# A feed-forward residual formed on token rows by GpSimd and added by VectorE in a stream of encoder jobs

## The chip, the core and the metric

The kernel runs on one core of one Trainium2 chip. The core has a matrix engine (TensorE, "PE" in the profile, with its weight loads as "PEld"), a vector engine (VectorE, "DVE"), a scalar engine (ScalarE, "ACT"), a general engine (GpSimd, "POOL") and a queue that only issues transfers (SyncE, "SP"). Products land in PSUM, which this part of the kernel uses as eight banks of 128 x 512 float32. The metric is the device time of one execution in microseconds (us); less is better. Before the change it is 2834.29 us, the median of three runs (2834.08 to 2835.43).

## The reference, cut to what matters

The reference is a chain of sixteen residual blocks on 2048 tokens of width 128, which the kernel holds as 8 images of 256 rows. The change touches one kind of block, `_L3_ffn_ref`, which is applied twice, once before and once after a sliding-window attention. It is a mixture of four encoder layers, of which a gate picks two for each image:

```python
def _encoder_layer(x, iw, ib, ow, ob, l1w, l1b, l2w, l2b, n1w, n1b, n2w, n2b):
    qkv = x @ iw.T + ib
    q, k, v = ...                      # 16 heads of width 8
    attn = softmax(q @ k.T / sqrt(8))
    o = (attn @ v) @ ow.T + ob
    x = _layernorm(x + o, n1w, n1b)
    ff = relu(x @ l1w.T + l1b) @ l2w.T + l2b
    return _layernorm(x + ff, n2w, n2b)
gate_logits = x.mean(axis=1) @ gate_w.T + gate_b
# the two best experts per image, weighted by the softmax over all four
return einsum('be,ebsd->bsd', gate_weights * mask, expert_outs)
```

The residual in question is the `x + ff` of the last line of `_encoder_layer`, where `x` is the normalised and scaled output of the first layer norm.

## The kernel before

**Jobs and passes.** `tail` runs the last stages as one stream, a `StripAttention`. Its queue holds 40 jobs: 16 encoder jobs (8 images x 2 experts), 8 window-attention jobs, 16 encoder jobs again. Attention over 16 heads is done in four strips of query columns, and the stream advances in passes, `s = 0, 1, 2, ...`, four per job. `burst(s)` issues, for the job of pass `s`, the four score tiles (`ps_s`, one per group of 32 rows, line 154), and for the strip two passes back the four weight tiles (`ps_t`, line 154). They go in two halves: two score and two weight tiles first, then the other two of each. Every tile is a bank of PSUM of 512 columns, taken from one ring of eight (`sml`), and it is written in two column blocks: the program lists the first blocks of all four tiles of a half, then the second blocks. After each half come the row maxima of its score tiles on VectorE (`top`, line 178, written to `nsp`) and the exponentials of its weight tiles on ScalarE (line 201, written to `g_pt`).

**Hooks.** All other work is hung on a pass with an order number and is issued after the pass's tiles in that order: the value product of an earlier strip (`av`, `ps_o`, order 1), the projections q, k, v of jobs ahead (`ps_q`, `ps_k`, `ps_v`, order 3), the normalisation (`half`, order 6), and last `lower` (order 9), which turns the maxima (`ps_m`) and adds them to the queries on VectorE (`qa`, line 209). A job begins at pass `4n`; its attention output is normalised seven passes later, and its feed-forward part runs beside the attention of the next jobs.

**Order.** In this stage the four compute engines keep the order in which the program issues their instructions (`manual_schedule`). What the planner still decides is which of the eight banks a tile takes, and it adds the semaphore waits that follow: a tile that takes a bank waits for the last reader of the tile that held it.

**The feed-forward part** is `ExpertFeed`, with these hooks for job `i` (pass counted from the job's first, order in brackets):

- 6 (0) `fetch`, line 818: gathers `g_ring` (the two weight matrices) and `g_RC` (263 columns of vectors) from device memory by an indirect transfer that GpSimd issues.
- 10 (0) `first_roots`: statistics of the first norm on VectorE, roots on GpSimd; 11 (8) `norm`: ScalarE writes the normalised rows `gxh`.
- 12 (5) `turn`, lines 858 to 870: TensorE turns `gxh` (`g_t`), ScalarE scales it to `gy` (features on partitions, line 866), and GpSimd adds the second bias to it as `gyr` (line 869).
- 13 and 14 (7) `up`: `g_h` = first weights x `gy` (line 876), ScalarE's ReLU to `g_hs`.
- 15 and 16 (7) `down`, lines 884 to 899: for each half of the rows, `g_f` is accumulated from an identity product of `gyr` (line 888), which puts the residual in, and four products of `g_hs` (line 892). ScalarE copies it out to `g_tt` (line 899).
- 16 and 17 (0) `second_roots`, lines 901 to 911: VectorE's statistics of `g_tt` (lines 904, 905) and its scaling (line 906), then roots on GpSimd. 18 (8) `settle`, lines 913 to 920: GpSimd weighs the result and adds it to `x`.

`open_` in `encoder_job` gathers the attention's weights `g_A` and vectors `g_RA`, both at once, at order 0 six passes before the job (for the first four jobs, at hooks of the stage before). `ps_q` needs `g_A` two passes later.

Of the kernel before, what the change touches and what calls it, by code (L numbers as in the profile page):

```python
# [15 lines left out]
ALU = mybir.AluOpType  # L16
# [3 lines left out]
P = 128  # L20
D = 128
B = 8
T = 256
# [786 lines left out]
class ExpertFeed:  # L810
# [4 lines left out]
    def tile(self, shape, name, bufs=2):  # L815
        return self.net.sa.wk.tile(shape, F32, tag=name, name=name, bufs=bufs)

    def fetch(self, i):
        w = self.net.gring[:, i % 4, :]
        self.gather_rows(None, "g_B", i, out=w)  # L820
        self.st[i] = dict(w=w, r=self.gather_rows(self.net.sa.wk, "g_RC", i, 4))

    def roots(self, mv, name, wi=None):
        nc = self.nc
# [34 lines left out]
    def turn(self, i):  # L859
        nc, d = self.nc, self.st[i]  # L860
        r = d["r"]
        ps = self.net.sml("g_t")
        for u in range(2):
            nc.tensor.transpose(ps[:, u * P : (u + 1) * P], d["xh"][:, u, :], self.net.ident)
        d["y"], d["yr"] = self.tile([P, T], "gy"), self.tile([P, T], "gyr")
        nc.scalar.activation(
            d["y"], ps[:, :T], AF.Identity, bias=r[:, 261:262], scale=r[:, 260:261]
        )
        nc.gpsimd.tensor_scalar(d["yr"], d["y"], r[:, 262:263], None, ALU.add)
        d["h"] = self.tile([P, 4, T], "g_hs")  # L870

    def up(self, i, a):
# [11 lines left out]
    def down(self, i, u):  # L884
        net, nc, d = self.net, self.nc, self.st[i]
        ps = net.sml("g_f")
        sl = slice(u * P, (u + 1) * P)
        nc.tensor.matmul(
            out=ps[:, :D], lhsT=d["yr"][:, sl], rhs=net.ident, start=True, stop=False
        )  # L890
        for j in range(4):
            nc.tensor.matmul(  # L892
                out=ps[:, :D], lhsT=d["h"][:, j, sl], rhs=d["w"][:, 512 + j * D : 512 + (j + 1) * D],
                start=False, stop=j == 3,
            )
        if u == 0:
            d["st"], d["mv"] = self.tile([P, 2, 6], "g_st2", 2), self.tile([P, 2, 2], "g_mv2", 2)
            d["t"] = self.tile([P, 2, D], "g_tt", 3)
        nc.scalar.copy(d["t"][:, u, :], ps[:, :D])

    def second_roots(self, i, u):
        nc, d = self.nc, self.st[i]
        mv, t = d["mv"], d["t"][:, u, :]
        nc.vector.bn_stats(out=d["st"][:, u, :], in_=t)
        nc.vector.bn_aggr(out=mv[:, u, :], in_=d["st"][:, u, :])
        nc.vector.scalar_tensor_tensor(
            t, t, mv[:, u, 0:1], d["r"][:, 0:D], ALU.subtract, ALU.mult
        )
        if u:
            d["rs"] = self.roots(mv, "g_rs2")  # L910
            nc.gpsimd.tensor_scalar(d["rs"], d["rs"], self.wf[:, i : i + 1], None, ALU.mult)
# [290 lines left out]
class Net:  # L1202
# [988 lines left out]
    def tail(self):  # L2191
        nc = self.nc
        pe = mybir.EngineType.PE
        with ExitStack() as es:
            rt = es.enter_context(self.tc.tile_pool(name="g_r", bufs=1))
            wg = es.enter_context(self.tc.tile_pool(name="g_w", bufs=4))
            gates = [Gate(self, rt, e) for e in range(2)]
            sa = self.sa = StripAttention(self, None, None)
            for i in range(2 * B):
                sa.add(self.encoder_job(wg, gates[0], i), i > 3)  # L2200
            hooks = []
            for b in range(B - 1):
                hooks += [
                    (8 * b + 16, self.ln_roots, b), (8 * b + 18, self.ln_apply, b),
                    (8 * b + 20, self.ln_turn, b),
                ]
            for b0, b1 in ((0, 2), (2, 5)):
                s = 8 * b1 + 13
                hooks.append((s, gates[0].means, b0, b1))
                hooks += [(s + 3, f) for f in gates[0].choose(b0, b1)]  # L2210
            for i in range(4):
                hooks.append((57 + 2 * i, sa.jobs[i].begin))
            with self.banks("h", 2, 4):
                self.layernorm_stats()
                with self.tc.tile_pool(name="h_k", bufs=2) as wk:
                    with self.tc.manual_schedule(engines={pe}):
                        WideAttention(self, wk, self.xnT).run(hooks)
            es.enter_context(self.banks("g", big=0, sml=8))
            wk = es.enter_context(self.tc.tile_pool(name="g_a", bufs=2))
            pts = [  # L2220
                self.w16.tile([P, 2, 4, 512], F32, tag="w16", name=f"g_pt{i}") for i in range(2)
            ]
            sa.wk, sa.weights = wk, lambda t: pts[t % 2][:, t // 2 % 2]
            self.gring = self.w16.tile([P, 4, 1024], F32, tag="w16", name="g_ring")
            es.enter_context(self.tc.manual_schedule(engines=INORDER))

            def gating(gate, s, b0, b1):
                sa.at(s, 0, gate.means, b0, b1)
                first, *rest = gate.choose(b0, b1)
                sa.at(s + 1, 5, first)  # L2230
                for k, f in enumerate(rest):
                    sa.at(s + 2 + k, 0, f)

            sa.at(-4, 0, self.ln_roots, B - 1)
            sa.at(-2, 0, self.ln_apply, B - 1)
            sa.at(-1, 5, self.ln_turn, B - 1)
            gating(gates[0], 0, 5, 8)
            for b in range(B):
                n = len(sa.jobs)
                sa.at(4 * n - 9, 0, self.ln_roots, b)  # L2240
                sa.at(4 * n - 8, 0, self.ln_apply, b)
                sa.at(4 * n - 6, 5, self.ln_turn, b)
                sa.add(self.window_job(wk, b))
                end = 4 * n + sa.AV["w"] + 7
                sa.at(end, 0, self.ln_roots, b)
                sa.at(end + 2, 0, self.ln_apply, b)
                sa.at(end + 3, 5, self.ln_turn, b)
                for b0, b1 in ((0, 2), (2, 5), (5, 8)):
                    if b1 == b + 1:
                        gating(gates[1], end + 4, b0, b1)  # L2250
            for i in range(2 * B):
                sa.add(self.encoder_job(wg, gates[1], i))
            sa.run()

    def window_job(self, wk, b):
# [15 lines left out]
    def encoder_job(self, wg, gate, i):  # L2271
        nc, b = self.nc, i // 2
        if gate.feed is None:
            gate.feed = ExpertFeed(self, gate)
        feed = gate.feed
        got = {}

        def open_():
            wa = got["wa"] = gate.gather(wg, "g_A", i, 4)
            ra = got["ra"] = gate.gather(wg, "g_RA", i, 4)  # L2280
            return (
                self.xnT[:, b, :], wa[:, 0:256], wa[:, 256:512], wa[:, 512:640], wa[:, 768:770],
                wa[:, 770:772], ra[:, 0:D],
            )

        def first(j):
            j.t = self.transpose2(j.wk, j.o, "oT8", self.nc.vector.tensor_copy)
            j.xr = j.wk.tile([P, 2, D], F32, tag="xr", name="xr")
            nc.gpsimd.tensor_tensor(
                j.xr, self.xn[:, 2 * b : 2 * b + 2, :],  # L2290
                got["ra"][:, D:].unsqueeze(1).to_broadcast([P, 2, D]), ALU.add,
            )

        def second(j):
            feed.add(i, j.xr, self.rowproj(j.t, got["wa"][:, 640:768], True))

        av = StripAttention.AV[None]
        hooks = [(av + 5, 4, first), (av + 6, 2, second)]
        for d, order, f, args in (
            (av + 3, 0, feed.fetch, ()), (av + 8, 8, feed.norm, ()), (av + 9, 5, feed.turn, ()),  # L2300
            (av + 10, 7, feed.up, (0,)), (av + 11, 7, feed.up, (1,)),
            (av + 12, 7, feed.down, (0,)), (av + 13, 7, feed.down, (1,)),
            (av + 7, 0, feed.first_roots, ()), (av + 13, 0, feed.second_roots, (0,)),
            (av + 14, 0, feed.second_roots, (1,)), (av + 15, 8, feed.settle, ()),
        ):
            hooks.append((d, order, lambda j, f=f, args=args: f(i, *args)))
        job = Job(None, 8 ** -0.5, open_, hooks)
        job.whole_q = True
        return job

    def resident(self):
# [85 lines left out]
def _cols(b):  # L2397
    return b.reshape(-1, P).T
# [6 lines left out]
def _layout(i):  # L2405
# [92 lines left out]
    for n in "qkv":  # L2498
# [11 lines left out]
    g = {n[len(p) :]: v for n, v in i.items() if n.startswith(p)}  # L2510
# [8 lines left out]
                axis=1,  # L2519
# [13 lines left out]
            for e in range(4)  # L2533
# [6 lines left out]
                [  # L2540
                    np.repeat(g["ln2_w"][e : e + 1], P, axis=0),
                    np.repeat(g["ln2_b"][e : e + 1], P, axis=0), _cols(g["lin1_b"][e]),
                    _cols(g["ln1_w"][e]), _cols(g["ln1_b"][e]), _cols(g["lin2_b"][e]),
                ],
                axis=1,
            )
            for e in range(4)
# [23 lines left out]
```

## Time and profile before

| What | Value |
|---|---|
| Median of three runs | 2834.29 us |
| The profiled execution: its own time, and its span | 2835.47 us, 2833.5 us |
| Granted TensorE clock, mean over the span | 0.943 |
| TensorE busy, whole span | 2485.3 us (88%) |
| VectorE, ScalarE, GpSimd busy, whole span | 1973.9, 1419.8, 1417.6 us |
| 1955 to 2270 us (first encoder stretch): TensorE, VectorE, ScalarE, GpSimd busy | 307.35, 235.46, 203.51, 184.67 us of 315 |
| 2270 to 2480 us (mostly window attention) | 194.99, 165.94, 118.84, 154.69 us of 210 |
| 2480 to 2834 us (second encoder stretch and the end) | 332.05, 248.56, 221.41, 219.12 us of 354 |

The profile is one execution, recorded instruction by instruction; the span is from its first to its last instruction. A row of the timeline or of a group names the line of the kernel, the engine, the operation, what is written and from what, and the shape. A bracket after a row is the time that the engine sat idle just before, with the instruction that ended the wait. Instructions of float32 matrix products appear twice per product. Ends of matrix products are modelled, so that the time of one is best read from the distance between starts.

### The profile page before, as it was taken

Reading aid. Unit: us, or ns where it says so; the run is one execution under the profiler, and the core shown is the slowest. Engines: PE = TensorE matmul, PEld = TensorE weight load, DVE = VectorE, ACT = ScalarE, POOL = GpSimd, SP = SyncE. Lnnn points to the kernel's source line nnn. Section 1 sums busy time; section 2 is a strip of 40 time slices with the busy share of each in tenths; the row PEclk is TensorE's granted clock in tenths of the full one; section 3 lists DMA queues with packets and bytes.
Section 4 is the critical chain, followed back from the end, with each engine's and each line's share of the span. In section 5 each row is a group of like instructions: output and inputs, shape, how many; then the busy total and the mean of one; then the engine's idle time right before and its main releaser. Section 6 shows DMA issues by size and latency. Waiting matters only on the chain.

```text
span 2833.5 us, 63773 instructions
## 1 busy us (share of the span) xinstructions
PE 2485.3 (88%) x25374; PEld 1779.3 (63%) x25374; DVE 1973.9 (70%) x4881; ACT 1419.8 (50%) x3300; POOL 1417.6 (50%) x1924
## 2 busy tenths in 40 slices
PE   6888769989689979795797599998999999999997
PEld 3444357756467767574465466675677777767775
DVE  5888856767757776553675377777777777887774
ACT  5666324446334343321563155554666665566664
POOL 3777559712198405222002244543466668746666
PEclk8999879999889989897898799999999999999998
DMA  3000000000000200003000300100121100012211
GB/s 106 1 1 1 33 1 1 1 1 2 3 1 1 88 3 2 1 27 47 5 2 33 45 1 1 31 1 1 45 69 52 53 30 3 25 52 63 64 56 35
DMA packets 41993, 69.99 MB, mean 25 GB/s; under 512 B 9176, under 2 KB 30561, under 8 KB 40929
## 3 DMA queue, kind: packets, MB, share of 16 engines
q0 software_dynamic: 12288, 42.14, 5.7%
q1 hardware_dynamic: 29408, 23.78, 2.7%
q8 instruction: 201, 3.29, 0.5%
q14 instruction: 96, 0.78, 0.1%
HBM read 58.82 MB, written 7.08 MB: 23 GB/s over the span
## 4 chain that ended last, share of the span: by engine, by line
PE 39%; DVE 5%; POOL 3%; DMA 1%; ACT 1%; issue 1%; POOLq 0%; ACTq 0%; DVEq 0%
PE ps_s L154 6%; PE ps_o L1475 5%; PE ps_t L154 5%; PE g_h L876 2%; PE h_o L502 2%; PE h_s L457 2%; PE h_t L487 2%; PE g_f L892 2%; PE h_p L416 2%; DVE nsp L178 2%; PE ps_m L207 1%; PE ps_ot L1485 1%; PE ps_q L1470 1%; PE ps_k L1470 1%; PE h_v L440 1%
## 5 line engine op out<-in xcount | busy, mean ns | idle before, releaser
L178 DVE TENSOR_REDUCE nsp<-ps_s 128x2 f32<-128x512 f32 x640 | 397.9, 684 | 91.6 <-PE ps_t L154 87.4
L154 PE MATMUL ps_t<-qa,k 32*128 32x256 f32 (+2 forms) x3584 | 423.1, 373 | 7.1 <-DVE qa L209 4.7
L154 PE MATMUL ps_s<-k,q 32*128 32x256 f32 (+2 forms) x3584 | 424.3, 375 | 0.5 <-DVE vaug L1460 0.3
L201 ACT ACTIVATE g_pt<-ps_t 128x512 f32<-128x512 f32 (+1 forms) x640 | 311.4, 570 | 160.5 <-PE ps_t L154 156.7
L154 PEld LDWEIGHTS ps_s<-k,q 32*128 32x128 f32 x3584 | 300.2, 187 | 55.4 <-issue 36.0
L154 PEld LDWEIGHTS ps_t<-qa,k 32*128 32x128 f32 x3584 | 316.2, 186 | 21.1 <-DVE qa L209 5.9
L475 POOL TENSOR_TENSOR hw<-hw,hden 128x512 f32<-128x512 f32 x128 | 130.3, 1040 | 164.9 <-DVE hden L472 116.7
L1118 POOL TENSOR_TENSOR h<-h,cs 128x512 f32<-128x512 f32 x128 | 164.5, 1306 | 84.7 <-DVE h L1117 81.9
L574 POOL TENSOR_SCALAR oh<-iota,f_tr 128x128 f32<-128x128 f32 (+1 forms) x256 | 137.1, 544 | 66.7 <-DVE f_tr L1682 32.1
L183 DVE TENSOR_REDUCE nsp<-ps_s 128x1 f32<-128x128 f32 (+2 forms) x512 | 132.6, 331 | 48.4 <-PE ps_t L154 39.4
L1475 PE MATMUL ps_o<-g_pt,vaug 128*32 128x256 f32 (+2 forms) x2816 | 161.9, 352 | 3.0 <-PE ps_s L154 2.6
L209 DVE TENSOR_TENSOR qa<-q,ps_m 128x256 f32<-128x256 f32 x224 | 93.7, 418 | 101.1 <-PE ps_m L207 93.1
L201 ACT ACTIVATE pt<-ps_t 128x384 f32<-128x384 f32 (+1 forms) x256 | 118.9, 551 | 85.3 <-PE ps_t L154 84.7
L1117 DVE TENSOR_TENSOR_SCAN h<-m_da,db 128x512 f32<-128x512 f32 x128 | 149.6, 1202 | 2.1 <-POOL m_ug L1021 1.4
L1129 PE MATMUL m_py<-h,ident 128*128 128x512 f32 x256 | 134.5, 632 | 13.5 <-POOL h L1118 11.7
L1384 PE MATMUL ln_ps<-ident,xn 128*128 128x128 f32 x256 | 61.4, 341 | 95.4 <-DVE xn L1376 90.2
L468 ACT ACTIVATE hw<-h_s,hm 128x256 f32<-128x256 f32 x256 | 117.7, 479 | 25.3 <-DVE hm L462 22.7
L1475 PEld LDWEIGHTS ps_o<-g_pt,vaug 128*32 128x32 f32 x2816 | 72.6, 110 | 73.8 <-DVE nsp L178 38.5
L99 POOL TENSOR_SCALAR q<-q8w,w_strip 128x256 f32<-128x256 f32 x96 | 87.2, 921 | 61.5 <-ACT q8w L95 57.4
L1111 ACT ACTIVATE m_da<-delta,m_a 128x510 f32<-128x510 f32 x128 | 87.6, 689 | 54.6 <-DVE h L1117 54.4
L1384 PEld LDWEIGHTS ln_ps<-ident,xn 128*128 128x128 f32 x256 | 36.1, 160 | 123.6 <-issue 78.4
L1515 POOL TENSOR_SCALAR_AFFINE_SELECT pt<-pt 128x512 f32<-128x512 f32 x64 | 39.1, 634 | 146.2 <-ACT pt L201 146.2
(503 smaller groups left out, 6499.0 us busy)
## 6 DMA issues: line engine op xcount, KB each, us to landing
mw<-in_e_w SPq DMA_DIRECT2D x2, 2048.0 KB, 8.5
moe_x<-e_bx SPq DMA_DIRECT2D x4, 640.0 KB, 4.6
e_bx<-moe_x SPq DMA_DIRECT2D x4, 640.0 KB, 4.8
x<-in_x SPq DMA_DIRECT2D x4, 256.0 KB, 3.8
fraw<-in_f_wq SPq DMA_DIRECT2D x1, 1024.0 KB, 6.8
fraw<-in_f_wk SPq DMA_DIRECT2D x1, 1024.0 KB, 8.8
w_f_wv<-in_f_wv SPq DMA_DIRECT2D x1, 1024.0 KB, 4.8
w_f_wout<-in_f_wout SPq DMA_DIRECT2D x1, 1024.0 KB
```

Source lines behind the costliest of these rows:

```text
L154: nc.tensor.matmul(**c)
L178: nc.vector.tensor_reduce(col, ps.rearrange("p (q k) -> p q k", q=2), AX.X, ALU.max, negate=True)
L183: nc.vector.tensor_reduce(col[:, qt : qt + 1], ps[:, c0 : c0 + nk], AX.X, ALU.max, negate=True)
L201: return lambda: nc.scalar.activation(out, ps[:, :width], AF.Exp, scale=j.scale)
L468: nc.scalar.activation(w[:, c], ps[:, c // 2, (c % 2) * T : (c % 2 + 1) * T], AF.Exp, bias=m[:, c : c + 1], accum_out=den[:, c : c + 1],)
L475: nc.gpsimd.tensor_tensor(w[:, sl], w[:, sl], den[:, sl].unsqueeze(2).to_broadcast([P, 2, T]), ALU.mult)
L574: pool.tensor_scalar(oh[:, t, lo : lo + n], net.iota[:, 0:n], slot, None, ALU.is_equal)
L1117: nc.vector.tensor_tensor_scan(h, da, db, 0.0, ALU.mult, ALU.add)
L1118: nc.gpsimd.tensor_tensor(h, h, cs, ALU.mult)
L1129: nc.tensor.matmul(out=self.py[k], lhsT=self.net.ident, rhs=h, start=n == 0, stop=n == 15)
L1384: self.nc.tensor.transpose(ps[:, u * P : (u + 1) * P], self.xn[:, 2 * b + u, :], self.ident)
L1475: self.nc.tensor.matmul(out=po[32 * i : 32 * i + 32, q0 : q0 + nq], lhsT=va[:, kt, h0 + i, :], rhs=pt[:, i, c0 : c0 + nq], start=n == 0, s ...
```

## The change

1. The residual is formed on token rows. `turn` no longer adds the bias to `gy`; GpSimd sums two bias rows to `g_row`, multiplies the normalised rows `gxh` with the first norm's scale row, and adds `g_row`, which gives `gyr` as 128 x 2 x 128 (tokens on partitions). For this, `g_RC` carries three full rows in place of one column, 646 columns instead of 263.
2. `down` has no identity product. Its four products stay in PSUM; there is no copy by ScalarE.
3. `second_roots` begins with an addition on VectorE of `gyr` and the PSUM tile, one pass after `down`.
4. The gathers are taken apart into four hooks at order 10, the last of a pass. Counted from a job's first pass: `g_A` at -7, `g_RA` at -5 (both at -6, order 0, before), `g_ring` at 6 (order 0 before), `g_RC` at 8 (order 0 at 6 before).

```diff
-    def fetch(self, i):
+    def fetch_w(self, i):
         w = self.net.gring[:, i % 4, :]
         self.gather_rows(None, "g_B", i, out=w)
-        self.st[i] = dict(w=w, r=self.gather_rows(self.net.sa.wk, "g_RC", i, 4))
+        self.st[i] = dict(w=w)
+
+    def fetch_r(self, i):
+        self.st[i]["r"] = self.gather_rows(self.net.sa.wk, "g_RC", i, 4)
...
-        d["y"], d["yr"] = self.tile([P, T], "gy"), self.tile([P, T], "gyr")
+        d["y"], d["yr"] = self.tile([P, T], "gy"), self.tile([P, 2, D], "gyr")
         nc.scalar.activation(
             d["y"], ps[:, :T], AF.Identity, bias=r[:, 261:262], scale=r[:, 260:261]
         )
-        nc.gpsimd.tensor_scalar(d["yr"], d["y"], r[:, 262:263], None, ALU.add)
+        wide = lambda c: r[:, c : c + D].unsqueeze(1).to_broadcast([P, 2, D])
+        row = self.tile([P, D], "g_row")
+        nc.gpsimd.tensor_tensor(row, r[:, 390:518], r[:, 518:646], ALU.add)
+        nc.gpsimd.tensor_tensor(d["yr"], d["xh"], wide(262), ALU.mult)
+        nc.gpsimd.tensor_tensor(
+            d["yr"], d["yr"], row.unsqueeze(1).to_broadcast([P, 2, D]), ALU.add
+        )
...
-        nc.tensor.matmul(
-            out=ps[:, :D], lhsT=d["yr"][:, sl], rhs=net.ident, start=True, stop=False
-        )
         for j in range(4):
             nc.tensor.matmul(
                 out=ps[:, :D], lhsT=d["h"][:, j, sl], rhs=d["w"][:, 512 + j * D : 512 + (j + 1) * D],
-                start=False, stop=j == 3,
+                start=j == 0, stop=j == 3,
             )
...
-        nc.scalar.copy(d["t"][:, u, :], ps[:, :D])
+        d["ps", u] = ps
 
     def second_roots(self, i, u):
         nc, d = self.nc, self.st[i]
         mv, t = d["mv"], d["t"][:, u, :]
+        nc.vector.tensor_tensor(t, d["yr"][:, u, :], d.pop(("ps", u))[:, :D], ALU.add)
         nc.vector.bn_stats(out=d["st"][:, u, :], in_=t)
...
             for i in range(2 * B):
-                sa.add(self.encoder_job(wg, gates[0], i), i > 3)
+                sa.add(self.encoder_job(wg, gates[0], i), False)
+                if i > 3:
+                    sa.at(4 * i - 7, 10, sa.jobs[i].fetch[0])
+                    sa.at(4 * i - 5, 10, sa.jobs[i].fetch[1])
...
-        def open_():
-            wa = got["wa"] = gate.gather(wg, "g_A", i, 4)
-            ra = got["ra"] = gate.gather(wg, "g_RA", i, 4)
-            return (
+        def fetch_a():
+            got["wa"] = gate.gather(wg, "g_A", i, 4)
+
+        def fetch_ra():
+            got["ra"] = gate.gather(wg, "g_RA", i, 4)
+            wa = got["wa"]
+            job.fill(
...
-            (av + 3, 0, feed.fetch, ()), (av + 8, 8, feed.norm, ()), (av + 9, 5, feed.turn, ()),
+            (av + 3, 10, feed.fetch_w, ()), (av + 5, 10, feed.fetch_r, ()), (av + 8, 8, feed.norm, ()), (av + 9, 5, feed.turn, ()),
```

The second encoder stretch is hooked in the same way, and the host-side layout adds the three rows to `g_RC`.

More of the change, by code (lines that the diff above doesn't have):

```diff
@@ L2211, in tail @@
             for i in range(4):
-                hooks.append((57 + 2 * i, sa.jobs[i].begin))
+                hooks += [(57 + 2 * i + k, sa.jobs[i].fetch[k]) for k in range(2)]
             with self.banks("h", 2, 4):
@@ L2251, in tail @@
             for i in range(2 * B):
-                sa.add(self.encoder_job(wg, gates[1], i))
+                n = len(sa.jobs)
+                sa.add(self.encoder_job(wg, gates[1], i), False)
+                sa.at(4 * n - 7, 10, sa.jobs[n].fetch[0])
+                sa.at(4 * n - 5, 10, sa.jobs[n].fetch[1])
             sa.run()
@@ L2276, in encoder_job @@
         got = {}
-        def open_():
-            wa = got["wa"] = gate.gather(wg, "g_A", i, 4)
-            ra = got["ra"] = gate.gather(wg, "g_RA", i, 4)
-            return (
+        def fetch_a():
[4 more added lines that the diff above has]
+            job.fill(
                 self.xnT[:, b, :], wa[:, 0:256], wa[:, 256:512], wa[:, 512:640], wa[:, 768:770],
-                wa[:, 770:772], ra[:, 0:D],
+                wa[:, 770:772], got["ra"][:, 0:D],
             )
@@ L2306, in encoder_job @@
             hooks.append((d, order, lambda j, f=f, args=args: f(i, *args)))
-        job = Job(None, 8 ** -0.5, open_, hooks)
+        job = Job(None, 8 ** -0.5, None, hooks)
         job.whole_q = True
+        job.fetch = fetch_a, fetch_ra
         return job
@@ L2542, in _layout @@
                     np.repeat(g["ln2_b"][e : e + 1], P, axis=0), _cols(g["lin1_b"][e]),
-                    _cols(g["ln1_w"][e]), _cols(g["ln1_b"][e]), _cols(g["lin2_b"][e]),
-                ],
+                    _cols(g["ln1_w"][e]), _cols(g["ln1_b"][e]),
+                ]
+                + [np.repeat(g[n][e : e + 1], P, axis=0) for n in ("ln1_w", "ln1_b", "lin2_b")],
                 axis=1,
```

## The prediction

> **What bounds the kernel now.** I read the page's span and slices first, then busy time per job in the stage that changes, then the timeline of one pass in it.
>
> ```profile
> span 2833.5 us, 63773 instructions
> ...
> PE   6888769989689979795797599998999999999997
> ...
> DVE  5888856767757776553675377777777777887774
> ```
>
> Each digit is a slice of 70.8 us. The change lies in the last twelve slices, from about 1980 us. TensorE (PE) fills nine tenths or more of nearly all of them.
>
> ```profile
> core 0: us, PE busy (x) PEld busy (x) DVE busy (x) ACT busy (x) POOL busy (x), PEclk, DMA share, GB/s
> ...
> 2580.96:2602.16 21.20, 21.20 (x308) 15.66 (x312) 15.79 (x38) 14.44 (x34) 14.29 (x22) 1.00 0.21 64
> ```
>
> This window is one encoder job: four passes in 21.20 us. TensorE has no gap. VectorE (DVE) works 15.79 us of it, ScalarE (ACT) 14.44 and GpSimd (POOL) 14.29. So a TensorE microsecond removed or added here is a microsecond of the kernel, and 5.4 us of VectorE and 6.9 us of GpSimd are free per job, where their places allow.
>
> Now one pass, with the second feed-forward product of an earlier job behind it (columns: start, duration, engine, line; in brackets the idle before):
>
> ```profile
> 2600.03 0.27 ACT L899 COPY g_tt<-g_f 128x128 f32<-128x128 f32 x1 [1.55 <-PE g_f L892]
> ...
> 2600.15 0.48 PE L154 MATMUL ps_s<-k,q 32*128 32x256 f32 x2
> ...
> 2600.25 0.42 DVE L209 TENSOR_TENSOR qa<-q,ps_m 128x256 f32<-128x256 f32 x1 [0.70 <-PE ps_m L207]
> ...
> 2601.13 0.38 PE L154 MATMUL ps_s<-k,q 32*128 32x256 f32 x2
> ...
> 2601.31 2.48 DVE L178 TENSOR_REDUCE nsp<-ps_s 128x2 f32<-128x512 f32 x4 [0.64 <-PE ps_t L154]
> ...
> 2601.78 0.38 PE L154 MATMUL ps_s<-k,q 32*128 32x256 f32 x2
> ...
> 2602.08 0.59 PEld L1475 LDWEIGHTS ps_o<-g_pt,vaug 128*32 128x32 f32 x16 [0.33 <-DVE nsp L178]
> 2602.09 1.07 PE L1475 MATMUL ps_o<-g_pt,vaug 128*32 128x256 f32 x16
> ...
> 2603.71 0.28 DVE L904 BATCH_NORM_STATS2 g_st<-g_tt 128x6 f32<-128x128 f32 x1
> ...
> 2604.44 0.39 PE L888 MATMUL g_f<-ident,gyr 128*128 128x128 f32 x2
> ...
> 2604.67 1.06 PE L892 MATMUL g_f<-g_ring,g_hs 128*128 128x128 f32 x8
> ```
>
> The reader should see three things. First, eight banks of PSUM are just enough: a pass takes a bank for each of its eight score and weight tiles and a ninth for ps_o, and ps_o already waits for VectorE's first row maximum (nsp) to give a bank back. That maximum ends at 2601.31 + 2.48/4 = 2601.93; ps_o starts 0.16 later. Second, the tiles go in two halves, 2600.15 to about 2601.13 and 2601.13 to 2601.99, the second half two rounds of 0.43. Third, g_f's bank is given back at 2600.30 by ScalarE's copy, before the second half needs it.
>
> **Part 1, identity products removed.** Per job two, of two PE instructions each. The one above runs from 2604.44 to 2604.67, 0.23; the ten instructions up to the next product at 2605.56 take 1.12, 0.112 each, so one product is 0.224. 64 of them: **-14.3 us**. All but the last four lie where TensorE is full.
>
> **Part 2, the evacuation moves from ScalarE to VectorE, one pass later.** The work is small:
>
> ```profile
> L899 ACT COPY g_tt<-g_f 128x128 f32<-128x128 f32 x64 | 17.1, 267 | 58.7 <-PE g_f L892 58.7
> ...
> L1499 DVE TENSOR_TENSOR o<-ps_ot,rc 128x128 f32<-128x128 f32 x112 | 32.5, 290 | 3.4
> ```
>
> ScalarE loses 0.27, VectorE gains 0.29 per half (same shape, one PSUM input), 0.58 per job, in front of the statistics. In the two passes concerned VectorE idles 1.04 before the next qa and 0.63 before the next maxima: hidden, if it is alone.
>
> What is not hidden is the bank. The add stands behind the next pass's four maxima in VectorE's queue, so g_f keeps its bank from the end of one pass to about 2604 in the next, 3.7 us longer, and that pass has seven banks. I read the built order of both kernels with the bank of each tile and what each wait names. Before: in none of the 230 passes does a tile of the second half wait for a tile of its own pass. After: in **56** passes the last weight tile (the fourth of the second half) takes the bank of the pass's own first score tile, and waits for its maximum. 48 are encoder passes (12 jobs x 2 in each of the two encoder stretches), 8 are in the window stretch between.
>
> Price: the release is the one ps_o waits for today, so the weight tile's first round starts at 2602.09 instead of about 2601.13. Queued behind it on TensorE are the second-round products of all four tiles, then ps_o. Two rounds remain, 2 x 0.43, so ps_o starts at 2602.95 instead of 2602.09: **+0.86**. After that nothing is late: the second maximum, which now frees ps_o's bank, ends 0.62 after the first, before 2602.95; the third and fourth shift 0.15; the exponentials have slack. No row shows this stall. From below 0.43 (ps_o could begin while the last round drains), from above 0.96 (the whole displacement of the tile) + 0.1 for a weight load no longer run ahead. I take 0.86, the count of rounds, less 0.06 for small gaps behind ps_o that can absorb some: 0.80 x 48 = 38.4. In the window passes the first maximum is shorter; the same count gives 0.72 in two (256 columns) and 0.54 in six (192 + 128): 4.7. Together **+43.1 us**.
>
> **Part 3, GpSimd.** It loses one operation and gains three.
>
> ```profile
> L869 POOL TENSOR_SCALAR gyr<-gy,g_RC 128x256 f32<-128x256 f32 x32 | 29.9, 934 | 9.1 <-ACT gy L866 9.1
> ...
> L2289 POOL TENSOR_TENSOR xr<-xn,g_RA 128x256 f32<-128x256 f32 x32 | 23.1, 723 | 0.0
> ```
>
> Two wide ones at 0.723 and a row sum of half the width, between 0.36 (half) and 0.62 (the 128x128 row of g_tb), say 0.45: 1.90 - 0.93 = +0.97 per job. The residual is needed one whole job later, 21 us, and GpSimd has 6.9 us free: nothing. Here the rule of the Trainium skill's "GPSIMD Engine Reference", section 4.1 (put adds of tiles on VectorE; GpSimd is about twice as slow with two inputs) speaks against the change. The rows give 0.723 against 0.415 for a 128x256 add on VectorE, 1.7 times; were it on the path it would be 0.97 x 32 = +31 us. The idle time decides: 0. A second rule, "SBUF — State Buffer", section "Who interferes with whom", says a VectorE operation with two SBUF inputs blocks against a GpSimd one reading SBUF. The new add reads PSUM and one SBUF tile, so it is exempt; L906 (two SBUF inputs) is not, and its rows run from 350 to 840 ns. At worst 0.49 against 0.34 of idle left (0.63 - 0.29): +0.15 per job, +5 us. I take 0 and keep 5 for the range.
>
> **Part 4, gathers.** All four stay on GpSimd's queue, at about 1 us each plus 0.3; no other queue is passed. g_A is third in a row of four today, behind g_ring and g_RC and behind roots that wait for VectorE; it now goes alone, a pass boundary earlier in the queue.
>
> ```profile
> 2517.50 1.07 PE L1470 MATMUL ps_q<-xnT,g_A 128*32 128x256 f32 x16 [2.17 <-DMA g_A<-in_g_A,g_idx]
> ```
>
> TensorE waits for it five times, 5.8 us in all. Two issues fewer in front are 2.6 us, more than the longest wait: **-5.8 us** (between 0 and -5.8). g_RC grows from 263 to 646 columns, 0.2 MB more per job; DMA is at 0.21 and the row is needed four passes later: 0. After the last passes GpSimd is itself on the chain (it runs without idle from 2805.7 into the last norms); there the two rounds of +0.97, less what the shorter product chain gives back, are **+1 us**.
>
> **Sum:** -14.3 + 43.1 - 5.8 + 1 = +24.0. The profiled execution took 2835.47 (span 2833.5 and 2.0 around it); it becomes 2859.5. The median of the runs, 2834.29, is 1.2 below it: **2858**.
>
> **Rivals.**
> - *The bank wait costs little* (other side): if ps_o did not set the pass's end, or the last tile overlapped it, 14.3 + 5.8 - 1 = 19 us are gained: 2815. It decides below 19/56 = 0.34 per pass. For it: ps_o needs the exponentials of an earlier pass only. Against: TensorE has no gap per job, and ps_o starts 0.16 after the very release.
> - *Half absorbed:* 0.45 per pass, +25 - 19 = +6: 2840.
> - *GpSimd and VectorE block each other:* two blocked operations of 0.49 per job ahead of the maxima, 31 us on top: 2889. Against: median of L906 is 352.
> - *The change does not do it on the chip:* the waits are in the program, so only their length is open.
>
> **Chances.** Main case 0.72, from 2843 (0.52 per pass) to 2876 (1.06, gathers bring half); bank wait free 0.11; half absorbed 0.10; blocking 0.07. For 8 in 10 I reach from 2839 to 2879. A difference of 0.2%, 5.7 us, is what a measurement can tell: faster 0.12, same 0.04, slower 0.84.
>
> **What would show it.** Identity product gone, PE instructions fewer by 128. In the pass after each g_f, the fourth weight tile of the second half waits on nsp, with ps_o 0.8 later, while the two other passes of a job keep their lengths; a job takes 21.2 - 0.45 + 1.6 = 22.4 us instead of 21.2. No PE wait on g_A. VectorE's maxima unchanged. Wrong, if a job takes 20.8 (no stall), or if all four passes grow (VectorE or GpSimd).

## The result, and the profile after

The changed kernel takes **2873.72 us**, the median of four runs (2869.96 to 2876.89), beside 2834.86 us for the kernel before in the same set of runs (median of four, 2834.08 to 2841.33). The ratio is 1.0131, 95% interval 1.0118 to 1.0143: slower by 38.9 us. The profiled execution took 2874.34 us, its span is 39.0 us longer than that of before.

The head of the page of the changed kernel, with the busy tenths of TensorE in 40 slices:

```profile
span 2872.5 us, 63595 instructions
...
PE   6888679989699878775996599998999999999997
```

There are 178 instructions fewer in sum. TensorE has 128 matrix instructions fewer, those of the identity products (25246 where it had 25374). The slices of the last stage look as full as before; that the stage has become slower isn't seen at this scale. It is seen in a table of one window, the job at the same place in the stream (from one `ps_o` to the fourth after it; columns: window, its length, busy time of each engine, granted clock, share of DMA, GB/s):

```profile
2605.52:2628.33 22.81, 22.14 (x302) 15.77 (x301) 16.66 (x40) 14.33 (x32) 15.19 (x23) 1.00 0.19 62
```

A job takes 22.81 us where it took 21.20. VectorE has 0.87 us more to do in it and GpSimd 0.90 more, and neither is near the length of the job. TensorE now has gaps, 0.67 us of them in the record. The starts of `ps_o` divide the job into its four passes. First before, then after:

```profile
2580.89 1.07 PE L1475 MATMUL ps_o<-g_pt,vaug 128*32 128x256 f32 x16
...
2586.61 1.07 PE L1475 MATMUL ps_o<-g_pt,vaug 128*32 128x256 f32 x16
...
2591.27 1.07 PE L1475 MATMUL ps_o<-g_pt,vaug 128*32 128x256 f32 x16
...
2596.79 1.07 PE L1475 MATMUL ps_o<-g_pt,vaug 128*32 128x256 f32 x16
...
2602.09 1.07 PE L1475 MATMUL ps_o<-g_pt,vaug 128*32 128x256 f32 x16
```

```profile
2605.52 1.07 PE L1482 MATMUL ps_o<-g_pt,vaug 128*32 128x256 f32 x16
...
2612.05 1.07 PE L1482 MATMUL ps_o<-g_pt,vaug 128*32 128x256 f32 x16
...
2616.70 1.07 PE L1482 MATMUL ps_o<-g_pt,vaug 128*32 128x256 f32 x16
...
2622.22 1.07 PE L1482 MATMUL ps_o<-g_pt,vaug 128*32 128x256 f32 x16
...
2628.33 1.07 PE L1482 MATMUL ps_o<-g_pt,vaug 128*32 128x256 f32 x16
```

The passes are 6.53, 4.65, 5.52 and 6.11 us, where they were 5.72, 4.66, 5.52 and 5.30. Two passes grew by 0.81 us each, and these are the two that follow a `g_f`; the other two kept their lengths to 0.01 us.

The timeline of one such pass of the changed kernel, to be laid beside the one in the prediction:

```profile
2625.36 0.48 PE L154 MATMUL ps_s<-k,q 32*128 32x256 f32 x2
...
2626.52 1.29 DVE L178 TENSOR_REDUCE nsp<-ps_s 128x2 f32<-128x512 f32 x2 [0.57 <-PE ps_t L154]
...
2627.27 0.48 PE L154 MATMUL ps_t<-qa,k 32*128 32x256 f32 x1 [0.33 <-DVE nsp L178]
...
2627.60 0.38 PE L154 MATMUL ps_s<-k,q 32*128 32x256 f32 x2
...
2628.02 1.29 DVE L178 TENSOR_REDUCE nsp<-ps_s 128x2 f32<-128x512 f32 x2 [0.21 <-PE ps_t L154]
...
2628.33 1.07 PE L1482 MATMUL ps_o<-g_pt,vaug 128*32 128x256 f32 x16
...
2629.22 0.28 DVE L910 TENSOR_TENSOR g_tt<-gyr,g_f 128x128 f32<-128x128 f32 x1
```

The second half of the tiles stops until the first row maximum is done (2626.52 + 1.29/2 = 2627.17) and goes on 0.10 later, with the idle time put down to `nsp`. VectorE's four maxima, one block of 2.48 us before, are torn into two pairs, since the third score tile is late. The bank that is missing is, by the built order that the prediction read, `g_f`'s, which the addition of line 910 gives back only at 2629.50. The list of TensorE's waits in the last stage has the same as a sum (columns: total us, times, longest):

```profile
PE ps_t L154 <- DVE nsp L178: 15.8, 48, 0.3
```

It happens 48 times, as many as there are passes with a late `g_f` whose scores are those of an encoder job. (In the window stretch the maxima are taken at line 183.) The 0.33 us in the bracket is not the price: the products before the stop are drawn with modelled ends, so the price is read from the distance between starts. From the first score product to `ps_o` it is 2.97 us here and 1.94 before, **1.03 us**, of which 0.22 come back as the identity product that the pass no longer has.

No wait of TensorE on `g_A` is left. The addition itself is cheap:

```profile
L910 DVE TENSOR_TENSOR g_tt<-gyr,g_f 128x128 f32<-128x128 f32 x64 | 17.8, 278 | 9.8 <-PE g_f L898 9.5 <-PE ps_tr L1539 0.3
```

### The profile page after: what moved, and what is told of

It reads as the page before. It is cut to its first block, busy times and chain, and to the rows that moved or that the text cites. A ratio compares the mean times of both kernels' runs of the same rounds, so it can differ in the third digit from the quotient of the medians.

```text
span 2872.5 us, 63595 instructions
## 1 busy us (share of the span) xinstructions
PE 2510.2 (87%) x25246; PEld 1783.8 (62%) x25246; DVE 2000.3 (70%) x4945; ACT 1415.0 (49%) x3236; POOL 1447.8 (50%) x1988
## 4 chain that ended last, share of the span: by engine, by line
PE 38%; DVE 6%; POOL 4%; ACT 1%; issue 1%; DMA 1%; POOLq 0%; ACTq 0%; DVEq 0%
PE ps_s L154 6%; PE ps_o L1482 5%; PE ps_t L154 5%; DVE nsp L178 2%; PE h_o L502 2%; PE g_h L885 2%; PE h_s L457 2%; PE h_t L487 2%; PE g_f L898 2%; PE h_p L416 2%; POOL g_pt L1522 1%; PE ps_ot L1492 1%; PE ps_m L207 1%; PE ps_k L1477 1%; PE ps_q L1477 1%
## 5 line engine op out<-in xcount | busy, mean ns | idle before, releaser
L154 PE MATMUL ps_t<-qa,k 32*128 32x256 f32 (+2 forms) x3584 | 458.9, 375 | 28.6 <-DVE nsp L178 15.8
L154 PE MATMUL ps_s<-k,q 32*128 32x256 f32 (+2 forms) x3584 | 437.5, 377 | 0.3 <-issue 0.2
L154 PEld LDWEIGHTS ps_t<-qa,k 32*128 32x128 f32 x3584 | 330.3, 185 | 64.7 <-DVE nsp L178 35.1
```

Of the source, the lines that this page charges most:

```text
L154: nc.tensor.matmul(**c)
```

## Experiments

The experiments fall into four sets of runs (the "calls" of the expectations), each on a chip of its own and each with runs of the kernel before beside it. A ratio below is to those of its own set. A difference between two times of different sets is between two chips.

**The bank given back earlier, in two ways.** The first has ScalarE copy `g_f` out in its own pass, as before the change, and VectorE add from the copy:

```diff
 def down(self, i, u):
...
-        d["ps", u] = ps
+        nc.scalar.copy(d["t"][:, u, :], ps[:, :D])
...
 def second_roots(self, i, u):
...
-        nc.vector.tensor_tensor(t, d["yr"][:, u, :], d.pop(("ps", u))[:, :D], ALU.add)
+        nc.vector.tensor_tensor(t, d["yr"][:, u, :], t, ALU.add)
```

> The changed kernel with ScalarE's copy out of PSUM put back at the end of the same pass; the addition of the residual stays on VectorE one pass later, now from the copy in SBUF. In its built order no pass has a weight tile that waits for a maximum of its own pass (0 of 56). Bank theory: the whole loss goes, and the product and gather gains remain: 2834.9 - 14.3 - 5.8 + 1 = 2816, range 2811 to 2822; one encoder job 20.75 us. Rival, that the added work on VectorE and GpSimd is what costs: the work is all still here, with one more ScalarE copy, so the time stays above 2860.

The second leaves the change as it is, and issues VectorE's addition in the pass of the products:

```diff
 def down(self, i, u):
...
-        d["ps", u] = ps
+        nc.vector.tensor_tensor(d["t"][:, u, :], d["yr"][:, u, :], ps[:, :D], ALU.add)
...
 def second_roots(self, i, u):
...
-        nc.vector.tensor_tensor(t, d["yr"][:, u, :], d.pop(("ps", u))[:, :D], ALU.add)
```

> The changed kernel with the addition of the residual issued on VectorE right after the four products, in the same pass, ahead of the turn of the maxima. No copy. In its built order 0 of 56 passes wait for a maximum of their own. Bank theory: as e1, 2816, range 2811 to 2824 (VectorE may hold qa back by some 0.1 us where it waits for the product). Rival, added work on VectorE and GpSimd: stays above 2860. If e2 is well below e1, ScalarE's copy had a cost too.

Measured: 2825.32 us (2818.99 to 2829.00) and 2825.51 us (2822.51 to 2826.91), 48.4 and 48.2 us less than the changed kernel. The job at the same place in the stream of the second:

```profile
2575.65:2596.41 20.76, 20.76 (x305) 15.22 (x301) 16.34 (x40) 14.38 (x32) 15.16 (x23) 1.00 0.22 66
```

TensorE has no gap again, with nearly the same work on VectorE and GpSimd as in the changed kernel. So it is the moment at which the bank comes back, not the work of the addition. Compared pass by pass, the changed kernel is longer by 0.90 to 1.03 us in 49 passes, 49.8 us together, and by 0.71 in three more. Two of the 49 (0.95 each) and two of the three lie in the window stretch.

**The gathers alone.** The kernel before with the four gathers of a job in four steps, as the change has them, and nothing else:

```diff
-            (av + 3, 0, feed.fetch, ()),
+            (av + 3, 10, feed.fetch_w, ()), (av + 5, 10, feed.fetch_r, ()),
...
+                    sa.at(4 * i - 7, 10, sa.jobs[i].fetch[0])
+                    sa.at(4 * i - 5, 10, sa.jobs[i].fetch[1])
```

> The kernel before with only the gathers taken apart into four hooks; identity product, ScalarE copy and the 263-column vectors as before. By the prediction's part 4: 2834.9 - 5.8 = 2829, range 2827 to 2835; no wait of TensorE on g_A. Rival, that the gathers themselves cost (the stage begins some 1 us later in the profile of the changed kernel): 2836 or more.

**The late bank alone.** The kernel before with ScalarE's copy of `g_f` moved to the next pass:

```diff
 def down(self, i, u):
...
-        nc.scalar.copy(d["t"][:, u, :], ps[:, :D])
+        d["ps", u] = ps
...
 def second_roots(self, i, u):
...
+        nc.scalar.copy(t, d.pop(("ps", u))[:, :D])
```

> The kernel before with one edit: ScalarE's copy of the second product is issued one pass later, behind that pass's exponentials. Identity product, GpSimd's work, VectorE's work and gathers as before; only the bank is held longer. In its built order 56 passes wait for a maximum of their own, as in the changed kernel. Bank theory, with the stall as the profile of the changed kernel shows it (0.80 per pass beside 0.22 of product removed, so 1.03): 2834.9 + 48 x 1.03 + 8 x 0.75 = 2890, range 2882 to 2896; with the 0.80 of the prediction 2878. Rival, added work: nothing is added, so 2835.

Measured: 2832.86 us (2827.56 to 2835.55) for the gathers and 2935.28 us (2931.82 to 2939.55) for the late copy, ratio 1.0183 (1.0166 to 1.0200). But the kernel before itself took 2882.69 us in this set (median of seven), 47.8 more than beside the result, so that the gathers alone compare as 0.9825 (0.9809 to 0.9841), and the two versions with the bank given back as 0.9799 (0.9781 to 0.9817) and 0.9804 (0.9788 to 0.9820). The sum of the late copy, 52.6 us over that, came near what was expected and is yet made up otherwise: the passes after the second `g_f` of a job grew from 5.73 to 6.75 us, by 1.03 as in the changed kernel, while those after the first went from 5.30 to 7.77. (The two such passes beside which only two gathers fall came at 6.33, again 1.03 more.) The 2.47 us are too much for the bank alone.

**Before and after once more.** Both kernels unchanged, in the second set.

> The kernel before, unchanged, for its own profile beside the others of this call: in the first call the kernel before took 2882.69 us where it had taken 2834.86 us beside the changed kernel, 47.8 us more, while the version of it with the four-step gathers alone took 2832.86 us. Theory A (the four gathers that before issues back to back hold up the pass that they fall into): if this chip is like that of the first call, the extra time lies in 31 to 33 passes that fall beside the gathers, some 1.4 us each (5.30 us becomes 6.75), and every other pass keeps its length (5.72, 4.65, 5.52 us). Theory B (the chip is slower as a whole): all passes are longer by 1.7%. If this chip is like that of the very first runs, 2835 us and nothing to be seen.

> The changed kernel, unchanged, beside the kernel before. Its gathers are apart, so theory A says 2872 us (2866 to 2879) on any chip: slower by 38 us where before takes 2835 us, and faster by 10 us where before takes 2883 us. Theory B (the chip as a whole) says a ratio of 1.013 on every chip: 2920 us where before takes 2883 us.

Measured: the kernel before 2883.24 us, and 2882.76 over all 25 runs of it in this set; the changed kernel 2875.85 us (2869.94 to 2882.61), ratio **0.9974** (0.9962 to 0.9986). The changed kernel is 2.1 us from its result, and the kernel before 48 us from its own: on this chip the change is faster by 0.26%. The passes say where: in the kernel before, one pass of 22 encoder jobs is about 7.30 us in place of 5.30, which makes 43.8 of the 48.4 us by which the stage is longer; the three others are mostly equal to 0.01 us. It is the pass into which the four gathers fall. (It is also the one of the late copy above: its 7.77 us are 0.47 more than this.) Its rows in the kernel before on this chip (the timelines of ScalarE, VectorE, TensorE and GpSimd, one after the other):

```profile
2632.59 1.09 ACT L201 ACTIVATE g_pt<-ps_t 128x512 f32<-128x512 f32 x2 [1.30 <-PE ps_ot L1485]
2635.55 0.37 ACT L218 COPY oT<-ps_o 128x256 f32<-128x256 f32 x1 [1.87 <-PE ps_m L207]
...
2635.61 0.26 DVE L1491 RECIPROCAL rc<-ps_ot 128x16 f32<-128x16 f32 x1 [2.52 <-PE ps_m L207]
...
2635.97 0.48 PE L154 MATMUL ps_t<-qa,k 32*128 32x256 f32 x1 [0.82 <-ACT oT L218]
...
2632.38 0.95 POOL L803 DMA_INDIRECT g_A<-in_g_A,g_idx  x1 [0.30 <-issue]
2633.63 0.95 POOL L803 DMA_INDIRECT g_RA<-in_g_RA,g_idx  x1 [0.30 <-issue]
```

ScalarE and VectorE stand still together until 2635.6. The products that they read next, `ps_o` and the first half of `ps_ot`, have modelled ends of 2631.91 and 2632.50, and TensorE goes on issuing until it needs the bank that ScalarE has not emptied. The trace also records when each engine signals that its work is done, and there the two are late: after 2632.55 TensorE gives no signal until 2635.52, and then five within 0.27 us, one each for `ps_o`, the two halves of `ps_ot`, `g_f` and `ps_m`. ScalarE starts 0.03 us after the first of the five, VectorE 0.03 after the second. In the kernel before beside the result the same five signals came within 0.04 us of the modelled ends. So both engines waited for TensorE, whose signal for `ps_o` came 3.6 us late; whether the products themselves were late or only their signals isn't told. (Of some 2110 signals of TensorE in the last stage, 207 come more than 0.3 us after the modelled end in this profile, and 5 in that one.) The transfers look alike on both chips; this is the window on this chip, and then the same place in the kernel before beside the result:

```profile
2632.50:2635.50 3.00, 2.65 (x22) 1.84 (x20) 0.58 (x1) 1.09 (x2) 2.65 (x4) 1.00 0.85 256
```

```profile
2577.20:2580.20 3.00, 3.00 (x41) 2.78 (x43) 1.60 (x7) 1.13 (x4) 2.65 (x4) 1.00 0.80 261
```

The DMA engines are as busy (0.85 and 0.80) and move as much, and GpSimd issues alike. VectorE does 0.58 us of work where it did 1.60. With the gathers in four steps, in the first set, this pass was 5.30 us and the kernel 2832.86: spreading them is worth 50 us where the standstill is, and 2 us against the kernel before beside the result, which ran on another chip. So theory A of the expectation has the place right, and the extra was 2.0 us a pass rather than 1.4; that the chip as a whole is slower is refuted by the equal passes.

**The identity products alone.** The kernel before without them:

```diff
-        nc.tensor.matmul(
-            out=ps[:, :D], lhsT=d["yr"][:, sl], rhs=net.ident, start=True, stop=False
-        )
...
-                start=False, stop=j == 3,
+                start=j == 0, stop=j == 3,
```

> The kernel before without the two identity products of a job: it leaves the residual of the feed-forward out of the sum (and still forms it on GpSimd), all else as before. Theory of the prediction (each product is 0.224 us of TensorE's chain, and nothing fills its place): 64 x 0.224 = 14.3 us less than the kernel before on the same chip, passes of 5.08 and 5.50 us in the place of 5.30 and 5.72 us. Rival (the time of the products was hidden by the maxima or the exponentials of the pass): 0 to 5 us less.

Measured, in the same set: 2884.21 us, ratio 1.0008 (0.9996 to 1.0021): nothing gained, where 14.3 us were expected. The pass with the second product of a job went from 5.72 to 5.50 us, as expected, 6.5 us over 29 passes. The one with the first stayed at 7.31: a product less on TensorE does not shorten the standstill. Single passes elsewhere were longer by 5.0 us together. The price of a product is therefore read from the two versions with the bank given back against the gathers alone: 0.22 us in 49 and 50 passes, 10.9 and 11.0 us.

**GpSimd's forming left out.** The version with the addition at once, without the three GpSimd operations:

```diff
-        d["y"], d["yr"] = self.tile([P, T], "gy"), self.tile([P, 2, D], "gyr")
+        d["y"], d["yr"] = self.tile([P, T], "gy"), d["xh"]
...
-        nc.gpsimd.tensor_tensor(row, r[:, 390:518], r[:, 518:646], ALU.add)
-        nc.gpsimd.tensor_tensor(d["yr"], d["xh"], wide(262), ALU.mult)
-        nc.gpsimd.tensor_tensor(
-            d["yr"], d["yr"], row.unsqueeze(1).to_broadcast([P, 2, D]), ALU.add
-        )
```

> The changed kernel with VectorE's addition moved up into the pass of the products (as in the version that took 2825.51 us) and without the three GpSimd instructions that form the residual on token rows: VectorE adds the normalised rows, so the residual's weight and its two offsets are left out of the result. 1.87 us of GpSimd a job fall away, some 60 us in all. Theory (GpSimd's forming is hidden): 2824 us, within 3 us of the version with the forming, and a job of 20.75 us as there. Rival (GpSimd's work holds VectorE up through the memory they share, or makes the residual late): 8 to 30 us less than it.

Measured: 2814.78 us (2811.25 to 2820.03), 10.7 us less than with the forming, which ran on another chip. That is in the range of the rival, but the jobs don't bear the rival out:

```profile
2564.14:2584.90 20.76, 20.76 (x303) 15.22 (x300) 16.18 (x40) 14.38 (x32) 13.56 (x20) 1.00 0.20 65
```

GpSimd works 1.60 us less, and the job is as long to 0.01 us. Between the two profiled executions, 5.8 us lie ahead of the stage, in code that neither touches (the stage begins between 1973.6 and 1985.8 us in the profiles of this study), and 5.5 in it. Of these, 3.4 are in three window passes, in two of which the version with the forming ran at a lower TensorE clock (a granted 0.60 in the longest, 0.88 in the one before it; more on this below), and 1.5 in three passes at the beginning of the two encoder stretches. So the forming costs nothing in a job; up to some 2 us outside can be its doing, and how much of the rest of the 10.7 is chance stays open.

**How many gathers, and where.** Three more orders of the gathers in the kernel before, by the pass (counted from the job's first) and the order number of their hooks:

| Version | `g_A` | `g_RA` | `g_ring` | `g_RC` |
|---|---|---|---|---|
| before | -6 (0) | -6 (0) | 6 (0) | 6 (0) |
| four together, one step earlier | -7 (10) | -7 (10) | 5 (10) | 5 (10) |
| one and three | -7 (10) | -6 (0) | 6 (0) | 6 (0) |
| two and two | -7 (10) | -7 (10) | 6 (0) | 6 (0) |

(-6 for one job is the same pass as 6 for the third job before it.) As an edit, for the four together:

```diff
-                sa.add(self.encoder_job(wg, gates[0], i), i > 3)
+                sa.add(self.encoder_job(wg, gates[0], i), False)
+                if i > 3:
+                    sa.at(4 * i - 7, 10, sa.jobs[i].fetch[0])
+                    sa.at(4 * i - 7, 10, sa.jobs[i].fetch[1])
...
-            (av + 3, 0, feed.fetch, ()),
+            (av + 2, 10, feed.fetch_w, ()), (av + 2, 10, feed.fetch_r, ()),
```

> The kernel before with its four gathers of a job still one behind the other on GpSimd's queue, but issued one step earlier (ahead of the wait for the first normalisation). The profile of the kernel before on the second chip shows ScalarE and VectorE standing still together for 1.9 and 2.5 us while the four gathers are in flight, in the pass that grows from 5.30 to 7.30 us. Theory D (dose: too many gathers in flight at once hold the two engines up, wherever they are issued): the loss moves with them, a pass before the one that was 7.30 us grows by 1 to 2 us, the time stays within 20 us of the kernel before on the same chip (2865 to 2890 us). Theory P (place: only that pass has no slack for them): the loss is gone, 2833 us (2827 to 2838). If this chip shows no loss in the kernel before (2835 us), both say 2830 us.

> The kernel before with the gather of g_A alone issued one step earlier; the other three stay where they were, one behind the other. Theory D: three in flight hold the engines up less than four, a loss of 0.5 to 1.5 us a job, so 15 to 45 us over the version with four steps (2848 to 2878 us). Theory A (it is the gather of g_A, third in the queue and wanted in the same pass): no loss, 2833 us.

> The kernel before with its four gathers in two steps: g_A and g_RA one step earlier, the other two where they were. Theory D: two at a time are harmless, as the profile of the version with four steps shows it where two of its gathers fall behind one another: 2833 us (2827 to 2838). Rival (any two that follow each other cost something): 2845 us or more.

Measured: 2826.82, 2830.98 and 2833.16 us, ratios 0.9979 (0.9969 to 0.9989), 0.9988 (0.9976 to 1.0000) and 0.9989 (0.9975 to 1.0003). On the chip of this third set the kernel before took 2834.98 us, as beside the result, and in none of the three a pass grew (5.30 us where the gathers fall). With no loss there to be moved, the runs don't tell dose from place. The profile of the kernel before in the second set gives a hint: two passes beside which only `g_ring` and `g_RC` fall kept their lengths there (5.45 and 5.30 us), but a window pass with only `g_A` and `g_RA` took 5.95 us where it took 4.24 beside the result. So a loss does not need four. What an earlier `g_A` is worth there is small: 8.2 us with all four gathers earlier, 4.0 and 1.8 in the two others, whose intervals reach 1.

**The best version once more.** The addition at once, unchanged:

> The changed kernel with VectorE's addition in the pass of the products once more, unchanged, beside the kernel before on whatever chip this is, for the question whether it beats the kernel before where that one loses nothing at its gathers. Theory (its time does not depend on the chip, since its gathers are in four steps, and the stall is what made the changed kernel slow): 2825 us (2819 to 2830), so a ratio of 0.9965 (0.994 to 0.998) where the kernel before takes 2835 us and 0.980 where it takes 2883 us. Rival (the gain seen in the first call was the chip's alone): no faster than the kernel before where that takes 2835 us.

Measured, in the fourth set: 2826.67 us (2819.35 to 2829.28), ratio 0.9796 (0.9781 to 0.9811); the kernel before took 2883.84 us there. The time of this version agrees with that of the first set to 1.2 us. That it beats the kernel before on a chip without the standstill as well (2825.5 and 2826.7 against 2834.9 and 2835.0, 0.3%) rests on runs of different sets, since neither of its two sets had such a chip.

## Why the prediction was right in sign and 16 us short

| Step | Forecast, us | Measured, us | From |
|---|---|---|---|
| 1, identity products | -14.3 | -11.0 | addition at once against gathers alone, 50 passes |
| 2, bank, encoder passes | +38.4 | +48.6 | changed kernel against addition at once, 48 passes |
| 2, bank, window passes | +4.7 | +3.3 | the same, two passes of 0.95 and two of 0.71 |
| 3, GpSimd | 0 | 0 in a job | forming left out |
| 4, gathers | -5.8 | -6.2 | gathers alone against before, both profiles, whole stage |
| The end | +1 | +0.2 | after against before, behind the last `ps_o` |
| Sum | +24.0 | +34.9 | |

Single passes that belong to none of these leave -5.0 us in the comparison for the bank and +5.2 in that of the first row, which cancel. The two profiles of before and after differ by 34.8 us within the stage, first to last `ps_o`, by 0.2 behind it, and by 4.0 ahead of it, where nothing is changed and the profiles of this study scatter by 12. That is the 39.0 of the spans.

**Part 2 is the cause, at the place and with the wait that it named, and its size is what was off.** The forecast price of a pass was two rounds of 0.43 after the release, 0.86, less 0.06 for gaps. The tile starts 1.91 us into the pass, where 1.94 was forecast (2600.15 to 2602.09). But from the restart to `ps_o` it is 2628.33 - 2627.27 = 1.06 us, not 0.86. The two rounds of 0.43 are four steps of 0.215, the distance in the flow; the first step after a start is 0.33 (2627.27 to 2627.60), and the last one, to `ps_o`, is 0.31 (2628.02 to 2628.33). Both could be read before: a pass starts with a step of 0.32 there too (2600.15 to the row below), and its `ps_o` comes 0.31 after the last score product (2601.78 to 2602.09).

```profile
2600.47 0.38 PE L154 MATMUL ps_s<-k,q 32*128 32x256 f32 x2
```

And the 0.06 for gaps that could absorb some was not there. 1.06 - 0.03 is the 1.03 measured. The prediction's bound from above is 1.06 as well, but by luck: it was made of the tile's whole displacement and a weight load, and not of these steps. Over 48 passes the missing 0.23 is 11 us. In the window stretch the two passes forecast at 0.72 came at 0.95, the same 0.2 more; of the six forecast at 0.54 two came at 0.71, and in the others nothing clear of the waits that are there anyway is seen.

**Part 1** was right per product (0.22) and wrong in "all but the last four": in 14 of 64 passes of that comparison nothing of it shows. **Part 4** was right on the chip of the result: the waits on `g_A` are gone. Its 6.2 us hold single passes of two profiles from two chips; the medians of the two kernels are 2.0 us apart. What it could not see from one profile is that the same four gathers cost 48 us on three of the chips of this study. **Part 3**: the weighing of the rule on GpSimd against its idle time held. The rivals with a free bank (2815) and with half of it (2840) are refuted by the 1.03; the blocking of VectorE by GpSimd is too, since with the addition at once a job is as long with GpSimd's forming as without it (20.76 us). That two passes kept their lengths does not speak to it, because its place was the two that grew.

## What to carry to other kernels

Before an eviction (the copy of a product out of its bank) is moved to a later step or to a busier queue, count the banks that live at once and find which tile takes the bank that now comes late: here the wait cost 50 us, where the additions are 17.8 us of an engine with time to spare, and giving the bank back in the same pass turned 2873.7 into 2825.5. A stop in the middle of packed products costs more than the rounds that remain, so price it with the restart. And take the baseline on more than one chip: the same two kernels compare as 1.013 and as 0.997.

## What was not expected of the hardware

**The kernel before has two times.** It takes 2835 us in two sets of runs, that of the result and the third, and 2883 us in the three others, on different chips and steadily within each (2876.76 to 2888.74 over 25 runs in one), while the changed kernel, with its gathers in steps, agrees between a chip of each kind to 2.1 us. The loss is mostly in the passes where four gathers follow each other, with ScalarE and VectorE standing still for 1.9 and 2.5 us until the late signals of TensorE come. Why these are late, and why only in some sets, is open; each set had one chip, so that the chip and all else that differs between sets are not told apart.

**The TensorE clock fell in single passes after a wait that at other times left it alone.** The changed kernel has two profiles here. One pass of the window stretch in the one beside the result (columns of the window as above; the granted clock is the third number from the end):

```profile
2485.30:2491.06 5.76, 5.76 (x69) 4.75 (x69) 4.03 (x11) 1.81 (x5) 5.60 (x9) 0.70 0.01 3
```

The same pass in the other:

```profile
2485.49:2489.64 4.15, 4.15 (x69) 3.45 (x69) 3.77 (x11) 1.72 (x5) 4.06 (x7) 1.00 0.02 4
```

The same 69 products, in both after a wait of TensorE for `qa`, 1.56 and 1.48 us: at a granted clock of 0.70 in one profile and 1.00 in the other, 5.76 us against 4.15. The Trainium skill, "TensorE: Matmul & The Clock Gate", section "What's actually happening", says that the gate watches activity in windows of about 3.4 us that run on their own, whatever the kernel does; where a gap lies in the window would then decide, which fits, but no run here shows the windows. Its table asks for a whole idle window, though, and here the clock fell after a wait of half that length. Such a pass turns up once or twice in several of the profiles (also with ScalarE's copy and with the addition at once, and in the kernel before in the second set), at 0.60 to 0.74: a difference of two or three microseconds between two profiles of this kernel can be that and nothing else.
